# A four-layer scan network on one core: products of the preparation copied out one unit later, layer 1's steps at other units, and the product with C written over h in a ring of seven

## The chip, the cores and the metric

The kernel runs on one core of a Trainium2 chip. The time is that of the device, in microseconds (us), from the first to the last instruction of the core. A shorter time is better. The numbers before the change are the median of three runs; durations of single instructions come from one further execution taken by the hardware profiler.

Five engines work side by side, each through its own queue of instructions: TensorE (PE in the profile; PEld is its weight load), VectorE (DVE), ScalarE (ACT), GpSimd (POOL) and SyncE (SP), which here only issues transfers. An engine that must wait for another waits on a semaphore.

## What is computed

The input is x of shape (4, 64, 64, 192) in float32. Four layers are applied, each as x = x + layer(group norm of x). Layers 0 and 3 are two-dimensional state-space scans in four directions over 4096 positions of an image, layer 2 is a pair of Toeplitz products, and layer 1 holds four independent one-dimensional scans over lines of 64 positions: along rows and along columns, each forwards and backwards. The scan of layer 1, which is the part that the change touches most:

```python
def mamba_block(xs, in_w, cw, cb, xw, dtw, dtb, Alog, Dv, ow):
    N, L, _ = xs.shape
    xz = jnp.einsum('nlc,dc->nld', xs, in_w)
    u, z = jnp.split(xz, 2, axis=-1)
    ...
    uc = jax.lax.conv_general_dilated(u_pad, cw[:, None, :], (1,), 'VALID', feature_group_count=DI)
    uc = silu(uc + cb[None, :, None])
    ...
    x_dbl = jnp.einsum('nld,ed->nle', uc, xw)
    dt, Bp, Cp = jnp.split(x_dbl, [DT_RANK, DT_RANK + DS], axis=-1)
    delta = jax.nn.softplus(jnp.einsum('nlr,dr->nld', dt, dtw) + dtb)
    A = -jnp.exp(Alog)

    def step(h, inp):
        d_t, b_t, c_t, u_t = inp
        dA = jnp.exp(d_t[:, :, None] * A)
        h = dA * h + (d_t * u_t)[:, :, None] * b_t[:, None, :]
        y = jnp.einsum('nds,ns->nd', h, c_t)
        return (h, y)
    ...
    y = jnp.moveaxis(ys, 0, 1) + uc * Dv
    y = y * silu(z)
    return jnp.einsum('nld,cd->nlc', y, ow)
```

There are 384 inner channels (192 in layer 3) and 16 states for each. Layers 0 and 3 run the same recurrence over a whole image, after a two-dimensional convolution.

## The kernel before

**Jobs and units.** A job is one chunk of 512 positions of one image in one direction. Layers 0 and 1 have 128 jobs each, layer 3 has 128 of half the channels. A job is cut into units: 64 channels times 4 states fill 128 partitions with 2 x 512 values each. That gives 24 units a job in layers 0 and 1 and 12 in layer 3, 7680 in all. `TWO` and `ONE` give the order of the units (channel tile t, group of states p, half c).

**What a unit costs.** TensorE spreads (delta times u) times B into PSUM (tile `b`, line 351), from a transposed copy `dtuT` and diagonal matrices `diag` that ScalarE makes (line 305). ScalarE makes `dA` by two exponentials (line 374). VectorE runs the recurrence (line 384 in layer 1, two scans at line 391 in layers 0 and 3) into `h`. GpSimd multiplies `h` by C into `hc` (line 396). TensorE adds the states of `hc` into `y` in PSUM (line 414, four matmuls a unit, in two halves for each pair of units). For a few units, called direct (p = 3), GpSimd makes b itself (`bs`, line 324) in place of TensorE, and `dA` is written to PSUM.

**The order.** `run_jobs` writes out a program in steps i, one for each unit. In step i it feeds unit i + 2 (`feed`: b and dA), scans unit i (`scan`: recurrence, product with C, and in layers 0 and 3 a copy of the last column to `carry`), spreads B for direct unit i + 3, folds an earlier pair (`collect`), and then calls whatever `steps` holds for i. A scheduler turns the program into a fixed order for each engine, and an engine takes its instructions in that order. So an instruction that waits holds up all behind it on its engine.

**The steps** prepare the next jobs. Their places are counted from the job's first unit, so in layer 1 the step -24 falls on the first unit of the job before. In layer 1 a job has these: `load` (the chunk xn by SP, and a buffer for u), three `input_of` (product for u, first tap on ScalarE at line 778, three taps on VectorE at line 783, Silu on ScalarE at line 786), `project` (B, C and the rank of dt into `xd`, then to memory), `turn_b`, three `step_size` (delta before Softplus, line 249), `finish` (Softplus, line 253, and delta times u, line 254), `store`, three `turn` (transposes into dtuT, line 268), three `gate` (z with Silu, line 791), and two `out`. Each makes a product on TensorE in one of two PSUM buffers (`mm`) and has ScalarE or VectorE copy it out at once, in the same step. `gated` (lines 800 and 801) follows the last fold of a channel tile. ScalarE holds one table of functions; Exp, Silu and Softplus are here in three, so each Silu or Softplus between two exponentials costs two table loads.

**Buffers that matter.** `h` has 3 buffers and `hc` 5; `dA` has 3; `b` has 2 in PSUM; `mm` has 2; xn has 2 and u has 3. `plan` places the loads of C, B, delta and delta times u, up to 12 units ahead of their first reader, not before a unit at which their source is ready.

Of the kernel before, what the change touches and what calls it, by code (L numbers as in the profile page):

```python
# [19 lines left out]
T = 512  # L20
# [16 lines left out]
class Kernel:  # L37
# [66 lines left out]
    def run_jobs(self, jobs, pools):  # L104
# [15 lines left out]
        waiting = []  # L120
        for i in range(min(start, -EARLY), end):
# [4 lines left out]
            if 0 <= i < len(units):  # L126
                k, t, p, c = units[i]
                self.scan(jobs[k], t, p, c, pools)
# [9 lines left out]
            if todo:  # L138
                k, two, n = waiting.pop(0)
                self.collect(jobs[k], two, n, pools)  # L140
                if n and two[1][1] == LAST:
                    jobs[k]["add"](two[0][0])
            for step in steps.get(i, []):
                step()

    def plan(self, jobs, order, pools):
# [3 lines left out]
        for k, job in enumerate(jobs):  # L150
# [6 lines left out]
            for j, (t, p, c) in enumerate(order):  # L157
                i, g = k * len(order) + j, 2 * t + c
                direct = c in job["direct"].get(p, ())
                reads = [("c", p, i, when["project"] + 5), ("both", g, i - AHEAD, when["finish"] + near)]  # L160
                if direct:
                    reads += [("bc", p, i - EARLY, when["project"] + 5), ("dtu2", g, i - EARLY, dtu)]
                else:
                    reads.append(("diag", p, i - AHEAD, when["turn_b"] + 5))
# [26 lines left out]
    def prepare(self, job, pools):  # L191
# [4 lines left out]
        def project():  # L196
# [3 lines left out]
            for t in range(NT):  # L200
                for h in range(2):
# [3 lines left out]
                    )  # L205
            xd = job["xd"] = prep.tile([128, 256], F32, name="xd", bufs=1)
# [23 lines left out]

        def turn_b():
# [5 lines left out]
            nc.scalar.copy(bt.rearrange("p (h k) n -> p k h n", h=2), of)  # L237

        def step_size(t):
# [9 lines left out]
            nc.scalar.activation(job["delta"][:, t, :], dp[:P], AF.Identity, bias=w["dtb"][:, t : t + 1])  # L249

        def finish():
            delta = job["delta"]
            nc.scalar.activation(delta, delta, AF.Softplus)  # L253
            (nc.gpsimd if job["carry"] is None else nc.vector).tensor_mul(job["dtu"], delta, job["u"])  # L254
            if job["carry"] is not None:
                return
            job["deltas"] = self.bcd.tile([DI, T], F32, name="delta_dram")
            nc.scalar.dma_start(job["deltas"].rearrange("(t p) l -> p t l", p=P), delta)

        def turn(t):  # L260
# [3 lines left out]
            if P == 128:  # L264
                to = job["dtuT"][t] = prep.tile([128, NB, P], F32, name="dtuT", bufs=NT + 1)
            else:
                to = job["dtuT"][:, :, t * P : (t + 1) * P]
            nc.scalar.copy(to, ps)
# [108 lines left out]
    def scan(self, job, t, p, c, pools):  # L377
# [4 lines left out]
        h = pools["work"].tile([128, 2 * T], F32, name="h", bufs=3)  # L382
        if carry is None:
            nc.vector.tensor_tensor_scan(h[:, way], dA[:, way], b[:, way], 0.0, ALU.mult, ALU.add)  # L384
        else:
# [8 lines left out]
            nc.scalar.copy(carry[g, p], hn[:, :, 0 if rev else T - 1])  # L394
        hc = pools["work"].tile([128, 2 * T], F32, name="hc", bufs=5)
        nc.gpsimd.tensor_mul(hc, h, job["cbc"][p])  # L396
        job["done"][t, p, c] = hc

# [124 lines left out]
    def ss2d_scan(self, pre, u_d, y_d, P, NT, ways, A, dtb):  # L523
# [3 lines left out]
        with (  # L527
# [27 lines left out]
            for k, (col, rev) in sorted(enumerate(ways), key=lambda one: one[1]):  # L555
# [7 lines left out]
                for c in range(NCH - 1, -1, -1) if rev else range(NCH):  # L563
# [11 lines left out]
                    def add(t, job=job, col=col, rev=rev, s=s):  # L575
                        y, rows = job["y"][t], min(128, DI - t * 128)
                        if rows == 64:

                            both = work.tile([128, T], F32, name="out", bufs=3)
                            nc.scalar.copy(both, y)  # L580
                            y = mm.tile([64, T], F32, name="fold_ps", tag="mm")
                            nc.tensor.matmul(y, self.fold, both, start=True, stop=True)
                        out = work.tile([rows, T], F32, name="out", bufs=3)
                        if rev:
                            nc.vector.tensor_add(out, y, job["before"].pop(t))
                        else:
                            nc.scalar.copy(out, y)
                        nc.scalar.dma_start(y_d[col][t * 128 : t * 128 + rows, s], out)
# [151 lines left out]
    def mamba_job(self, pw, pin, mm, i, begin, rev, w, x, done, both_w, c, fixed, zero):  # L740
# [33 lines left out]
        def input_of(t):  # L774
# [3 lines left out]
            nc.scalar.activation(u, ps, AF.Identity, scale=tap(3))  # L778
            for j in range(1, 4):
                to, of = slice(j, HW), slice(0, HW - j)  # L780
                if rev:
                    to, of = of, to
                nc.vector.scalar_tensor_tensor(  # L783
                    u[:, :, to], ps[:, :, of], tap(3 - j), u[:, :, to], ALU.mult, ALU.add
                )
            nc.scalar.activation(u, u, AF.Silu, bias=w["conv_b"][:, t : t + 1])

        def gate(t):
            if t == 0:
                job["z"] = pin.tile([P, NT, T], F32, name="z")  # L790
            nc.scalar.activation(job["z"][:, t, :], project(t, DI, "z"), AF.Silu)
# [6 lines left out]
        def gated(t):  # L798
            u, z = job["u"][:, t, :], job["z"][:, t, :]
            nc.vector.scalar_tensor_tensor(u, u, w["D"][:, t : t + 1], job["y"][t], ALU.mult, ALU.add)  # L800
            nc.gpsimd.tensor_mul(z, z, u)
# [15 lines left out]
        def out(m):  # L817
# [9 lines left out]
            if rev:  # L827
                nc.vector.tensor_add(o, ps, o)
            else:
                nc.scalar.copy(o, ps)  # L830
            for rows, ch, at in parts(m):
                nc.sync.dma_start(done[ch, at], o[rows, :])

        when = dict(project=-24, turn_b=-22, step_size=(-20, -18, -17), finish=-15, turn=(-10, -7, -3), store=-11)
        each = lambda f, ats: [(at, lambda t=t: f(t)) for t, at in enumerate(ats)]
        steps = [(-50, weights)] if begin else []
        steps += [(-48, load)] + each(input_of, (-45, -32, -29)) + each(gate, (-6, -4, -2)) + each(out, (32, 35))
        if rev:
            steps += each(earlier, (26, 29))
# [328 lines left out]
```

## Time and profile before

| | us |
|---|---|
| median of three runs | 31623.03 |
| lowest and highest | 31622.8 and 31625.03 |
| the profiled execution | 31644.44 |
| its span, from first to last instruction | 31641.4 |
| layer 0: scans of one image (four of them) | 2270 |
| layer 1: all jobs | 11520 |
| layer 3: scans of one image (four of them) | 1285 |

The last three rows are stretches of the profiled execution. The rest of the span belongs to the inputs and outputs of layers 0 and 3 and to layer 2 (about 22290 to 25290), which the change leaves alone. A line of groups in the profile gives line, engine, operation, tiles and shapes, then the number of instructions; after the bar come the time in which the group was busy, the mean duration of one in ns, and the idle time of the engine just before them with what ended it. A line of waits gives who waited for whom: us in total, times, and the longest.

### The profile page before, as it was taken

To read this page: it belongs to the slowest core of one execution; us is meant where nothing else is said; L and a number is where in the kernel's file an instruction comes from. 1 tells how busy PE (TensorE), PEld (TensorE's weight loads), DVE (VectorE), ACT (ScalarE), POOL (GpSimd) and SP (SyncE) were. 2 spreads that over 40 slices of the span, in tenths; PEclk is the share of its full clock that TensorE was granted. 3 is DMA by queue.
4 is the path that set the end of the run, shared out by engine and by line. 5 is a ranking of instruction groups with operands and counts; after the bars stand their busy time and mean duration, and the time that the engine had idled before them with its cause. 6 is when DMAs were issued, how large, how long until landed. Compare 5 with 4: busy or idle time off the path is not lost.

```text
span 31641.4 us, 503746 instructions
## 1 busy us (share of the span) xinstructions
PE 27491.3 (87%) x189464; PEld 16459.4 (52%) x189464; DVE 22376.5 (71%) x16587; ACT 23377.2 (74%) x50388; POOL 22882.0 (72%) x9831
## 2 busy tenths in 40 slices
PE   8998998998899689888888998888588988888888
PEld 5654654665565355555555555555355344444444
DVE  7887887888888677776667777666423267777767
ACT  7885885886788488888878888878232187878777
POOL 7885885886788388888888888888100077777777
PEclk9999999999999899999999999999788999999999
DMA  3333334334333433333333333323533444444444
GB/s 107 103 98 115 103 99 119 99 97 112 106 101 99 135 95 95 95 96 93 95 95 95 94 94 96 94 93 94 129 78 77 104 128 126 128 126 129 126 129 125
DMA packets 1606619, 3342.23 MB, mean 106 GB/s; under 512 B 350645, under 2 KB 407414, under 8 KB 1588566
## 3 DMA queue, kind: packets, MB, share of 16 engines
q1 hardware_dynamic: 1432150, 3033.08, 35.4%
q10 hardware_dynamic: 172032, 276.92, 2.6%
q8 instruction: 1497, 24.53, 0.3%
q14 instruction: 940, 7.70, 0.1%
HBM read 2149.81 MB, written 656.08 MB: 89 GB/s over the span
## 4 chain that ended last, share of the span: by engine, by line
PE 32%; ACT 20%; DVE 15%; POOL 15%; DMA 9%; issue 8%; SPq 1%; ACTq 1%; DVEq 0%; POOLq 0%
PE b L351 12%; POOL hc L396 11%; ACT diag L305 7%; DVE h L391 7%; PE y L414 6%; ACT dA L374 5%; DVE h L384 3%; DMA xn<-m_col 2%; DMA xn<-m_row 2%; POOL bs L324 2%; PE yt_ps L1018 2%; ACT b L374 2%; DMA xn<-t_xn 2%; PE conv_ps L500 2%; POOL dtu L254 1%
## 5 line engine op out<-in xcount | busy, mean ns | idle before, releaser
L396 POOL TENSOR_TENSOR hc<-h,c 128x1024 f32<-128x1024 f32 x7680 | 18152.7, 2385 | 3279.0 <-DVE h L384 1520.9
L351 PE MATMUL b<-diag,dtuT 128*64 128x256 f32 x98304 | 13293.5, 389 | 1212.0 <-DVE h L391 720.5
L351 PEld LDWEIGHTS b<-diag,dtuT 128*64 128x64 f32 x98304 | 8701.4, 139 | 5531.3 <-issue 1840.9
L414 PE MATMUL y<-hc,fold 128*64 128x512 f32 x30720 | 10297.8, 604 | 918.1 <-POOL hc L396 896.8
L391 DVE TENSOR_TENSOR_SCAN h<-dA,carry,b 128x512 f32<-128x512 f32 x6720 | 8183.8, 1264 | 1482.5 <-PE b L351 779.6
L374 ACT ACTIVATE dA<-both,A 128x512 f32<-128x512 f32 (+1 forms) x12288 | 8333.1, 712 | 567.7 <-DVE h L384 551.8
L384 DVE TENSOR_TENSOR_SCAN h<-dA,b 128x1024 f32<-128x1024 f32 x2304 | 5244.7, 2282 | 2214.7 <-PE b L351 1011.0
L305 ACT ACTIVATE diag<-ident,bt 128x128 f32<-128x128 f32 x20480 | 6503.3, 390 | 138.6 <-issue 104.0
L414 PEld LDWEIGHTS y<-hc,fold 128*64 128x64 f32 x30720 | 3121.3, 138 | 3147.3 <-POOL hc L396 1904.1
L324 POOL TENSOR_TENSOR bs<-dtu,bc 128x1024 f32<-128x1024 f32 x1536 | 3640.1, 2370 | 169.7 <-DMA dtu<-dtu 73.0
L468 POOL MEMSET pad<- 128x13068 f32 (+1 forms) x8 | 73.4, 9172 | 3972.6 <-DMA cw<-in_L_conv_w 3003.3
L374 ACT ACTIVATE b<-both,A 128x504 f32<-128x504 f32 (+1 forms) x3072 | 2079.1, 677 | 368.8 <-DVE h L391 324.4
L384 DVE TENSOR_TENSOR_SCAN h<-b,bs 128x1024 f32<-128x1024 f32 x768 | 1752.9, 2282 | 287.9 <-ACT b L374 177.7
L394 ACT COPY carry<-h 128x2 f32<-128x2 f32 x4608 | 846.3, 184 | 1292.8 <-DVE h L391 1092.3
L391 DVE TENSOR_TENSOR_SCAN h<-b,carry,bs 128x512 f32<-128x512 f32 x1344 | 1640.8, 1262 | 210.7 <-ACT b L374 108.1
L783 DVE SCALAR_TENSOR_TENSOR u<-in_ps,conv_w,u 128x504 f32<-128x504 f32 (+2 forms) x1152 | 829.5, 720 | 946.4 <-ACT u L778 929.8
L226 PEld LDWEIGHTS dtu_ps<-ident,dtu 128*64 128x64 f32 (+1 forms) x16384 | 1185.7, 140 | 559.9 <-issue 283.7
L374 ACT ACT_TABLE_LOAD x1125 | 1443.4, 1283 | 18.2 <-DMA both<-delta_dram 4.0
L226 PE MATMUL dtu_ps<-ident,dtu 128*64 128x128 f32 (+1 forms) x16384 | 1374.4, 274 | 64.1 <-DVE dtu L254 41.6
L766 PE MATMUL in_ps<-xn,in_w 96*64 96x512 f32 x3072 | 1052.8, 626 | 390.5 <-DMA xn<-m_row 199.1
L391 DVE TENSOR_TENSOR_SCAN h<-dA,b 128x512 f32<-128x512 f32 x960 | 1113.7, 1205 | 363.3 <-ACT dA L374 134.5
L254 DVE TENSOR_TENSOR dtu<-delta,u 128x1536 f32<-128x1536 f32 (+1 forms) x256 | 571.3, 2232 | 572.4 <-ACT delta L253 572.2
(154 smaller groups left out, 23411.3 us busy)
## 6 DMA issues: line engine op xcount, KB each, us to landing
c<-bc_dram SPq DMA_DIRECT2D x3072, 256.0 KB
both<-delta SPq DMA_DIRECT2D x2048, 128.0 KB
bc<-bc_dram SPq DMA_DIRECT2D x768, 256.0 KB
both<-delta_dram SPq DMA_DIRECT2D x768, 256.0 KB
dtu<-dtu_dram SPq DMA_DIRECT2D x768, 256.0 KB
dtu<-dtu SPq DMA_DIRECT2D x1280, 128.0 KB
L_y<-out ACTq DMA_DIRECT2D x512, 256.0 KB
u<-L_u SPq DMA_DIRECT2D x160, 768.0 KB
```

The source lines that it names most:

```text
L226: nc.tensor.matmul(to[half * 64 : (half + 1) * 64], of[:, half * 64 : (half + 1) * 64], self.ident[:p, :p], start=True, stop=True,)
L254: (nc.gpsimd if job["carry"] is None else nc.vector).tensor_mul(job["dtu"], delta, job["u"])
L305: nc.scalar.activation(to, self.ident, AF.Copy, scale=of)
L324: self.nc.gpsimd.tensor_mul(by(b), dtu, by(job["bbc"][p]))
L351: nc.tensor.matmul(to, dtu, job["diag"][p][:, k, 2 * q : 2 * q + 2, :], start=True, stop=True,)
L374: nc.scalar.activation(to[n], of, AF.Exp, scale=w["A"][:, g, 2 * p + n : 2 * p + n + 1])
L384: nc.vector.tensor_tensor_scan(h[:, way], dA[:, way], b[:, way], 0.0, ALU.mult, ALU.add)
L391: nc.vector.tensor_tensor_scan(hn[:, n, way], dA[:, n, way], by_n[:, n, way], start, ALU.mult, ALU.add)
L394: nc.scalar.copy(carry[g, p], hn[:, :, 0 if rev else T - 1])
L396: nc.gpsimd.tensor_mul(hc, h, job["cbc"][p])
L414: nc.tensor.matmul(y[c * 64 : (c + 1) * 64, :], self.fold, of, start=first == 0 and n == 0, stop=last == LAST and n == 1)
L766: nc.tensor.matmul(ps[half * 64 : (half + 1) * 64, :], w["in_w"][:, k, first : first + 64], job["xn"][:, k, :], start=k == 0, stop=k == KC ...
```

## The change

1. A step may return a function, and `run_jobs` calls that one unit later. The steps of the preparation make their product in one unit and return the copy that takes it out of PSUM (in `input_of` the taps come one unit later, and the Silu one more). The carry copy of layers 0 and 3, the add of a finished y, and delta times u also move by one unit. `plan` counts C and B as ready one unit later.
2. In layer 1 the places change: `load` from -48 to -46, `input_of` from (-45, -32, -29) to (-37, -34, -31), `step_size` from (-20, -18, -17) to (-20, -19, -17), `turn` from (-10, -7, -3) to (-9, -2, 3), `gate` from (-6, -4, -2) to (-4, -1, 1), `out` from (32, 35) to (30, 33), `earlier` from (26, 29) to (25, 28).
3. In layer 1 the product with C is written over `h`, which has a ring of seven; `hc` with its five buffers is gone there. In layers 0 and 3 `h` and `hc` stay.

```diff
-        waiting = []
-        for i in range(min(start, -EARLY), end):
+        waiting, rest = [], []
+        for i in range(min(start, -EARLY), end + 4):
...
-                self.scan(jobs[k], t, p, c, pools)
+                after = self.scan(jobs[k], t, p, c, pools)
+                if after is not None:
+                    steps.setdefault(i + 1, []).insert(0, after)
...
-                    jobs[k]["add"](two[0][0])
-            for step in steps.get(i, []):
-                step()
+                    steps.setdefault(i, []).append(lambda job=jobs[k], t=two[0][0]: job["add"](t))
+            now, rest = rest + steps.pop(i, []), []
+            for step in now:
+                after = step()
+                if after is not None:
+                    rest.append(after)
...
             nc.scalar.activation(delta, delta, AF.Softplus)
-            (nc.gpsimd if job["carry"] is None else nc.vector).tensor_mul(job["dtu"], delta, job["u"])
...
+            def after():
+                (nc.gpsimd if job["carry"] is None else nc.vector).tensor_mul(job["dtu"], delta, job["u"])
+
+            return after
...
-        h = pools["work"].tile([128, 2 * T], F32, name="h", bufs=3)
+        h = pools["work"].tile([128, 2 * T], F32, name="h", bufs=7 if carry is None else 3)
...
-            nc.scalar.copy(carry[g, p], hn[:, :, 0 if rev else T - 1])
-        hc = pools["work"].tile([128, 2 * T], F32, name="hc", bufs=5)
+        hc = h if carry is None else pools["work"].tile([128, 2 * T], F32, name="hc", bufs=5)
         nc.gpsimd.tensor_mul(hc, h, job["cbc"][p])
         job["done"][t, p, c] = hc
+        if carry is None:
+            return None
+
+        def after():
+            nc.scalar.copy(carry[g, p], hn[:, :, 0 if rev else T - 1])
+
+        return after
...
+                        def halves():
                             both = work.tile([128, T], F32, name="out", bufs=3)
                             nc.scalar.copy(both, y)
...
+                            def sum_them():
+                                one = mm.tile([64, T], F32, name="fold_ps", tag="mm")
+                                nc.tensor.matmul(one, self.fold, both, start=True, stop=True)
+                                return lambda: last(one)
+
+                            return sum_them
+
+                        return halves if rows == 64 else last
...
-            nc.scalar.activation(u, ps, AF.Identity, scale=tap(3))
...
+            def taps():
+                nc.scalar.activation(u, ps, AF.Identity, scale=tap(3))
...
+                return last
+
+            def last():
+                nc.scalar.activation(u, u, AF.Silu, bias=w["conv_b"][:, t : t + 1])
+
+            return taps
...
-            nc.scalar.activation(job["z"][:, t, :], project(t, DI, "z"), AF.Silu)
+            ps = project(t, DI, "z")
+
+            def after():
+                if t == 0:
+                    job["z"] = pin.tile([P, NT, T], F32, name="z")
+                nc.scalar.activation(job["z"][:, t, :], ps, AF.Silu)
+
+            return after
...
-        when = dict(project=-24, turn_b=-22, step_size=(-20, -18, -17), finish=-15, turn=(-10, -7, -3), store=-11)
+        when = dict(project=-24, turn_b=-22, step_size=(-20, -19, -17), finish=-15, turn=(-9, -2, 3), store=-11)
...
-        steps += [(-48, load)] + each(input_of, (-45, -32, -29)) + each(gate, (-6, -4, -2)) + each(out, (32, 35))
+        steps += [(-46, load)] + each(input_of, (-37, -34, -31)) + each(gate, (-4, -1, 1)) + each(out, (30, 33))
         if rev:
-            steps += each(earlier, (26, 29))
+            steps += each(earlier, (25, 28))
```

## The prediction, made before the changed kernel had run

> **What bounds the kernel now.** I read the page first, then busy time in windows (one per layer), then the groups and the waits inside layer 1, then one job of layer 1 in order of time.
>
> ```profile
> span 31641.4 us, 503746 instructions
> PE 27491.3 (87%) x189464; PEld 16459.4 (52%) x189464; DVE 22376.5 (71%) x16587; ACT 23377.2 (74%) x50388; POOL 22882.0 (72%) x9831
> ```
>
> No engine fills the span, so the answer lies in the stages. The next lines are three windows: one of the four images of layer 0's scans, all of layer 1's, one image of layer 3's. Columns: window, length, busy time of PE, PEld, DVE, ACT, POOL, then granted clock, DMA share, GB/s.
>
> ```profile
> 189.00:2459.00 2270.00, 2121.34 (x16633) 1364.42 (x16629) 1957.55 (x1614) 1906.68 (x4711) 2017.30 (x863) 0.97 0.38 98
> 10770.00:22290.00 11520.00, 10195.31 (x69976) 6136.16 (x69974) 7978.45 (x4719) 9458.56 (x17176) 9860.38 (x4360) 0.97 0.30 94
> 25448.00:26733.00 1285.00, 1130.64 (x8130) 665.49 (x8126) 996.68 (x829) 1173.16 (x3002) 1146.79 (x479) 1.00 0.50 129
> ```
>
> Layer 1 is the largest single stage: 11520 us, 128 jobs, 90.0 us a job of 24 units. Its POOL is busy 9860 us, 77.0 a job, and idles 1660 us, 13.0 a job. Where that idle time comes from, by groups (first line) and by waits (the rest):
>
> ```profile
> L396 POOL TENSOR_TENSOR hc<-h,c 128x1024 f32<-128x1024 f32 x3072 | 7214.8, 2371 | 1598.2 <-DVE h L384 1520.9 <-DMA c<-bc_dram 64.4 <-PE b L351 7.2
> ...
> DVE h L384 <- PE b L351: 1011.0, 389, 11.7
> ACT u L778 <- PE in_ps L766: 923.6, 241, 14.2
> DVE u L783 <- ACT u L778: 898.5, 268, 14.6
> ...
> DVE h L384 <- POOL hc L396: 609.6, 417, 5.4
> ...
> DVE h L384 <- ACT dA L374: 538.8, 191, 8.7
> ```
>
> POOL waits for nothing but late scans. The scans are late because DVE stands behind a convolution tap (L783) that waits for ACT (L778), which waits for TensorE's product, or because dA is late on ACT. Yet DVE also waits 609.6 us for POOL: at other places it could run further ahead and the ring of three h forbids it. One job of POOL in order of time (start, length, what, in brackets the idle time before it) shows that the idle time is not spread:
>
> ```profile
> 16175.02 2.37 POOL L396 TENSOR_TENSOR hc<-h,c 128x1024 f32<-128x1024 f32 x1 [5.14 <-DVE h L384]
> ...
> 16190.50 2.36 POOL L396 TENSOR_TENSOR hc<-h,c 128x1024 f32<-128x1024 f32 x1 [3.81 <-DVE h L384]
> ...
> 16207.06 2.38 POOL L396 TENSOR_TENSOR hc<-h,c 128x1024 f32<-128x1024 f32 x1 [6.04 <-DVE h L384]
> ...
> 16214.62 11.69 POOL L396 TENSOR_TENSOR hc<-h,c 128x1024 f32<-128x1024 f32 x5
> ```
>
> These are units 21, 1 and 4; from unit 5 to unit 20 POOL never stops (five multiplies in 11.69 us, 2.34 each). Averaged over 124 jobs the idle time before POOL's work is 4.35 us at unit 21, 0.58 + 2.73 + 0.68 at units 0, 1 and 2 (and 0.41 before the gated multiply there), 3.29 + 0.45 at units 4 and 5, 0.20 at 9 and 10: 12.7 a job. So layer 1 is POOL-bound for two thirds of a job and has three holes in the rest.
>
> **What the skill says.** The Trainium skill, "ScalarE: Activation LUTs", section "What ACT_TABLE_LOAD costs", gives about 1283 ns for a table load and 1380 ns of drain. The trace agrees on the first (1283 in every load group) and shows no drain behind it: a load at 16257.88 of 1.28 us is followed by dA at 16259.17. "Perfetto Trace Analysis", section "Tensor Engine Instruction (MATMUL, LD_WEIGHTS)", says ACT, DVE and GpSimd take their instructions strictly in order; the 898.5 us of scans held behind L783 agree. "TensorE: Matmul & The Clock Gate", section "What's actually happening", says an array idle for some 3.4 us falls to half clock. At 16199.38 the first matmul after 4.10 us of waiting for xn takes 1.09 us where 0.59 is usual, so a DMA wait costs more than itself.
>
> **The change part by part.** The built order of both programs (it holds no times) tells what moves.
>
> 1. Chunk loaded 9 units ahead. Before, xn was loaded 3 units before its first product, about 11 us, and took 13.2 to 16.7 us in the chains. PE waited 376 us for it directly (190.5 + 185.3), and unit 4's hole is its shadow. After, load at unit 2 and product at unit 11: nine units at 3.3 us, 30 us. No byte is added; SP issues the same load one unit after the last product that reads the old chunk, so it blocks nothing new. 3.74 us a job fall to about 0.1: -3.6.
>
> 2. Steps spread. An excursion of ACT to another table costs two loads and the work: 2 x 1.28 + 0.60 to 0.72 = 3.2 us, six a job and one for Softplus (4.0). Before, in a job of the second direction, five stood between dA of unit 22.5 and 1.5 of the next job. In those three units ACT owed 16 us for them, 4.2 for dA (3 x 1.4), some 3.5 for diag and 1.2 for copies, 25 us, while POOL needed about 9. The 15 us of shortage less the lead (three dA buffers, 7 to 9 us) leave 6 to 8 us; the measured holes at 21 and 0 to 2 are 8.75. After, the excursions stand at 19, 21, 23 or 0, 2 or 3, and 5. Over those 10.5 units ACT owes 16 + 14.7 + 2.8 (copies) + 7.5 (diag), 41 us; POOL owes 10.5 x 2.34 + three bs at 2.33 + two z at 1.24, 34 us. Shortage 7, about the lead. Silus share a load somewhat more often: 2334 loads in all for 2395, 61 x 1.28 = 78 us of ACT, inside the lead. The first tap used to be ordered such that DVE waited for an ACT 1.5 to 2.5 units ahead; now 2.5, 1.5 and 0.5. I leave 1.0 of 4.35 at unit 21 and 2.0 of 4.40 at units 0 to 2: -5.7. Bounds: nothing regained, and all 8.75.
>
> 3. Evacuation in the next unit. 923.6 us of ACT and 898.5 of DVE idle in layer 1 are the same holes as in 1 and 2, so they are not counted again. Each product holds its PSUM buffer (two of them) a unit longer; products are at least a unit apart, so the third finds the first one free. Bounds: -0.5 to +1 us a job, taken at 0. The gated step and POOL's dtu (3.41 us) also move by one unit.
>
> 4. Ring of seven. The five hc buffers go and the scan of unit u+7 waits for TensorE's fold of unit u instead of the scan of u+3 for POOL's multiply of u. In the built order that fold comes after b of u+6 at the latest, which needs the scan of u+4, so it stands two scans clear. It lets DVE lead POOL by about four units instead of three, 2.3 us more cover at each hole; that is what makes the 1.0 and 2.0 above plausible. No work is added. Cost taken at 0.
>
> Second floor. TensorE's matmuls, counts by mean spacing in layer 1, owe 79.5 us a job (b 34.2, y 21.2, products for u and z 11.1, the rest 13.0). Part of that is the cold clock: granted 0.97, so 3% or 2.5 us, most of it behind the xn waits that go. That leaves some 77, as much as POOL's. Two engines in strict order that meet at every fold will not both be full: 0.7 us a job is given back.
>
> Layer 1: 3.6 + 5.7 - 0.7 = 8.6 us a job x 128 = -1100 us, 81.4 us a job against 77.0 of POOL.
>
> 5. Layers 0 and 3. In layer 0 the built order hardly changes: the scheduler already put the copies behind later dA, the DVE order is the same to the instruction, and its one hole (DVE's dtu behind Softplus at unit 11) stays. The carry copy moves behind dA of u+3, but that dA waits for the same scan (three dA buffers), so 256.9 us an image of ACT waiting for it mostly change their name: -20 in all. In layer 3 the halves' fold and last add move by one to three units; DVE waited 43.4 us an image for y and ACT 38.8 behind that. Half of the first: -20 x 4 = -80. Bounds for both layers: +150 to -350.
>
> Sum: -1100 - 20 - 80 = -1200. The profiled execution took 31644 us (span 31641.4 and 3 around it), so 30444; it lay 21 above the median of 31623, so **30420 us**.
>
> **Rivals.** (A) Only the DMA hole closes, because ACT's shortage of 7 us in a row uses up the lead and shows later: 3.6 x 128 = -460, and nothing elsewhere: 31160. For it: ACT's total work is not less. Against: POOL pauses for no ACT over units 5 to 20, where Softplus stands. (B) POOL never starves: 12.5 x 128 = -1600 and -200 in layers 0 and 3: 29820. Against: the second floor. (C) The ring makes it slower: the fold is the second half of a pair and queues behind b (1.73 us) and the first half (0.86), so DVE waits up to 2.6 us at each of 12 pairs. Above 0.7 us a pair this eats the whole gain; at 1.0, 12.0 - 8.6 = +3.4 x 128 less 100 elsewhere: 31960. For it: PEld already waits 893.3 us for hc at the fold. Against: the built order's clearance. (D) The scheduler undoes the spreading: no change. Against: the order shows it moved.
>
> **How the numbers follow.** Forecast 0.58 (30050 to 30800 for itself), A 0.20, B 0.12, C 0.07, D 0.03. The range leaves out C, D and the far edges of A and B: 29900 to 31080. Faster 0.90; within 0.2% (63 us, about what a measurement of this kernel can tell from none) 0.03; slower 0.07.
>
> **What would show it.** Right: in layer 1 POOL's idle time before its multiply falls from 1598 to about 550 us, PE waits for xn no more, the table-load groups of L374, L786 and L791 lie apart, a window of 1000 us there has POOL over 930, and layers 0 and 3 keep their lengths within 1%. Step 1 is wrong if a hole stays at unit 4; step 2 if holes move to units 14 to 16 behind Softplus; step 4 if scans wait for y. The prediction is wrong as a whole if layer 0 changes by more than 2%, since I give its order no effect.

## The result and the profile after

The kernel after takes 31289.92 us (median of 4; before 31624.03), a ratio of 0.9894 with a 95% interval of 0.9877 to 0.9911. The direction was forecast; the size was not: 334 us in place of 1200. The profiled execution has a span of 31282.5 us.

The windows of the kernel after, in the same three stages as before (columns: window, length, busy time of PE, PEld, DVE, ACT, POOL, granted clock, DMA share, GB/s):

```profile
189.00:2459.00 2270.00, 2110.20 (x16571) 1366.54 (x16567) 1948.03 (x1607) 1898.23 (x4702) 2009.32 (x859) 0.97 0.37 98
10794.00:21995.00 11201.00, 10189.22 (x69942) 5865.06 (x69942) 7953.58 (x4717) 9352.71 (x17118) 9860.85 (x4359) 0.97 0.31 97
25156.00:26427.00 1271.00, 1106.57 (x8137) 663.17 (x8134) 994.66 (x830) 1174.92 (x3002) 1149.32 (x480) 0.99 0.49 131
```

GpSimd (POOL) and TensorE are as busy in layer 1 as before; only idle time went. Measured from the first to the last multiply by C, the four images of layer 0 take 9115.0 us in sum (before 9080.3), layer 1 11188.6 (11507.3), layer 3 5072.6 (5142.4): +35, -319 and -70. All layer times below are read in this way. A job of layer 1 is timed from its first multiply to that of the next job, as the mean of 30 inner jobs of each way: the forward ways take 85.2 us a job (87.5 before), the backward ways 89.5 (92.1).

GpSimd's groups in layer 1, after; the idle time before each and its end stand behind the bar:

```profile
L418 POOL TENSOR_TENSOR h<-h,c 128x1024 f32<-128x1024 f32 x3072 | 7209.3, 2376 | 918.1 <-DVE h L407 570.0 <-DMA c<-bc_dram 284.0 <-PE b L374 26.9
L347 POOL TENSOR_TENSOR bs<-dtu,bc 128x1024 f32<-128x1024 f32 x768 | 1821.2, 2371 | 307.9 <-issue 224.8 <-DMA dtu<-dtu_dram 80.2 <-DMA c<-bc_dram 1.4
```

The multiply's idle time fell from 1598 to 918, where about 550 was forecast. The share that ends with a scan fell from 1521 to 570. But C's transfers now end 284 us of it (64 before), and the product bs, which hardly waited before (24 us), waits 308. The waits of layer 1 (us in total, times, longest) name the rest:

```profile
PEld y L443 <- POOL h L418: 1208.6, 704, 19.9
DVE h L407 <- PE b L374: 829.2, 688, 9.1
DVE h L407 <- ACT b L397: 790.9, 418, 3.1
...
DVE u L852 <- PE y L443: 659.2, 127, 10.8
...
ACT dA L397 <- DMA bc_dram<-xd: 337.4, 54, 8.4
ACT dtuT L289 <- PE dtu_ps L235: 286.4, 77, 5.3
```

No wait of TensorE for the chunk is left. In its place VectorE waits for dA of the direct units (b L397, 179 before), for the fold in the gate's sum (95 before), and ScalarE for transfers and for TensorE. One backward job of GpSimd in order of time shows where (start, length, idle time in brackets):

```profile
14510.68 4.72 POOL L418 TENSOR_TENSOR h<-h,c 128x1024 f32<-128x1024 f32 x2
14521.19 2.37 POOL L347 TENSOR_TENSOR bs<-dtu,bc 128x1024 f32<-128x1024 f32 x1 [5.80 <-issue]
14523.52 9.27 POOL L418 TENSOR_TENSOR h<-h,c 128x1024 f32<-128x1024 f32 x4
14536.60 1.27 POOL L853 TENSOR_TENSOR z<-z,u 128x512 f32<-128x512 f32 x1 [3.81 <-DVE u L852]
14540.01 2.36 POOL L418 TENSOR_TENSOR h<-h,c 128x1024 f32<-128x1024 f32 x1 [2.14 <-DMA c<-bc_dram]
```

The old holes at units 21, 1 and 4 closed, and others opened at 21 (before bs), 1 (before z) and 2. Over 30 jobs of a way: backward 4.4 us at unit 21 and 5.4 at unit 2; forward 1.4 at z of unit 1, 1.5 at unit 2, 4.6 at units 6, 7 and 9.

### The profile page after: what moved, and what is told of

Read it like the earlier page. It is cut to its first block, busy times and chain, and to the rows that moved or that the text cites. A ratio compares the mean times of both kernels' runs of the same rounds, so it can differ in the third digit from the quotient of the medians.

```text
span 31282.5 us, 503240 instructions
## 1 busy us (share of the span) xinstructions
PE 27353.4 (87%) x189464; PEld 16218.5 (52%) x189464; DVE 22344.0 (71%) x16587; ACT 23257.2 (74%) x50327; POOL 22884.2 (73%) x9831
## 5 line engine op out<-in xcount | busy, mean ns | idle before, releaser
L418 POOL TENSOR_TENSOR hc<-h,c 128x1024 f32<-128x1024 f32 x4608 | 10938.8, 2394 | 1641.9 <-DVE h L414 1336.6
L374 PEld LDWEIGHTS b<-diag,dtuT 128*64 128x64 f32 x98304 | 8544.2, 139 | 5362.7 <-issue 1770.1
L397 ACT ACTIVATE dA<-both,A 128x512 f32<-128x512 f32 (+1 forms) x12288 | 8308.5, 711 | 2062.3 <-DVE h L414 981.2
L418 POOL TENSOR_TENSOR h<-h,c 128x1024 f32<-128x1024 f32 x3072 | 7209.3, 2376 | 918.1 <-DVE h L407 570.0
L443 PE MATMUL y<-hc,fold 128*64 128x512 f32 x18432 | 5587.0, 605 | 534.0 <-POOL hc L418 533.3
L443 PE MATMUL y<-h,fold 128*64 128x512 f32 x12288 | 4736.9, 614 | 716.2 <-POOL h L418 713.0
L443 PEld LDWEIGHTS y<-hc,fold 128*64 128x64 f32 x18432 | 1709.8, 139 | 1684.1 <-POOL hc L418 978.7
L397 ACT ACTIVATE b<-both,A 128x504 f32<-128x504 f32 (+1 forms) x3072 | 2074.0, 675 | 527.9 <-DVE h L414 438.3
L443 PEld LDWEIGHTS y<-h,fold 128*64 128x64 f32 x12288 | 1321.9, 139 | 1804.2 <-POOL h L418 1210.7
L235 PE MATMUL dtu_ps<-ident,dtu 128*64 128x128 f32 (+1 forms) x16384 | 1309.6, 278 | 171.2 <-ACT z L839 125.3
```

Of the source, the lines that this page charges most:

```text
L235: nc.tensor.matmul(to[half * 64 : (half + 1) * 64], of[:, half * 64 : (half + 1) * 64], self.ident[:p, :p], start=True, stop=True,)
L374: nc.tensor.matmul(to, dtu, job["diag"][p][:, k, 2 * q : 2 * q + 2, :], start=True, stop=True,)
L397: nc.scalar.activation(to[n], of, AF.Exp, scale=w["A"][:, g, 2 * p + n : 2 * p + n + 1])
L443: nc.tensor.matmul(y[c * 64 : (c + 1) * 64, :], self.fold, of, start=first == 0 and n == 0, stop=last == LAST and n == 1)
```

## Experiments: the parts alone

Each run below is one part of the change alone, or the change without one part. Late evacuation means that a product is copied out of PSUM one unit later. Theory A: the change does what the forecast's steps say, and new waits at the new places take the gain. B: the ring couples VectorE to the fold. C: another part carries the gain (three h were short, or late evacuation).

e1_ring, the kernel before with

```
-        h = ... name="h", bufs=3)
+        h = ... name="h", bufs=7 if carry is None else 3)
-        hc = ... name="hc", bufs=5)
+        hc = h if carry is None else ... name="hc", bufs=5)
```

> The kernel before, with one part of the change alone: in layer 1 the product with C is written over h, in one ring of seven; places and evacuations stay old. Theory A (the change's gain was lost to new waits at the new places; the ring is neutral): all layers within 0.2%, layer 1 11507 +- 25 us, total 31560 to 31690. Theory B (the ring of seven couples VectorE to TensorE's fold, so scans wait for the fold): layer 1 longer by 100 us or more, total above 31720, and VectorE waits for y in layer 1. Theory C (h was short at three, the wait of VectorE for GpSimd, 610 us in the profile before, was real): layer 1 shorter by 150 us or more.

e2_places, the kernel before with the new `when`, `steps` and `earlier` numbers of layer 1 and nothing else:

> The kernel before, with layer 1's new places alone (chunk loaded 46 units ahead of its first scan and its first projection at 37, steps spread, out and earlier two or one units sooner); each product is still evacuated in its own unit, h and hc stay apart. Theory A (places take the old holes away and open new ones): layers 0 and 3 unchanged within 3 us an image; layer 1 shorter by 150 to 300 us; TensorE no longer waits for the chunk (376 us before), holes at units 2 and 21 of the backward ways appear. Theory B (ring at fault): layer 1 shorter by 450 us or more here, since the ring is absent. Theory C (late evacuation carries the gain): layer 1 changes by less than 100 us.

e3_late, the kernel after with those numbers and h, hc put back:

> The kernel after, with layer 1's old places and h (three) and hc (five) apart: of the change only the evacuation in the next unit is left, in all layers. Theory A: layer 0 longer by 35 us in sum and layer 3 shorter by 70 us in sum, as in the kernel after, since only this part touches them; layer 1 shorter by 0 to 150 us; total 31450 to 31600. Theory C (late evacuation carries layer 1's gain): layer 1 shorter by 250 us or more, total below 31360. Against both: layer 1 longer than before.

e4_noring, the kernel after with h (3) and hc (5) put back:

> The kernel after, with h (three) and hc (five) apart in layer 1: places and late evacuation stay, the ring is undone. Theory A (ring neutral): total 31260 to 31340, layer 1 within 40 us of 11189. Theory B (the ring holds the scans back): layer 1 shorter by 150 us or more, total below 31140. Theory C (three h were short): layer 1 longer by 150 us or more.

Measured (us; total is the median):

| kernel | total | layer 0 | layer 1 | layer 3 | forward / backward us a job |
|---|---|---|---|---|---|
| before | 31624 | 9080 | 11507 | 5142 | 87.5 / 92.1 |
| e1_ring | 31610 | 9075 | 11477 | 5146 | 87.2 / 91.9 |
| e2_places | 31240 | 9078 | 11106 | 5143 | 84.0 / 89.7 |
| e3_late | 31445 | 9112 | 11348 | 5068 | 88.3 / 88.8 |
| e4_noring | 31329 | 9109 | 11243 | 5067 | 86.2 / 89.4 |
| after | 31290 | 9115 | 11189 | 5073 | 85.2 / 89.5 |

Layer times come from one profiled execution each, and that of the kernel before lay 21 us above its median; beside the four runs the kernel before took 31613. The ring alone is therefore not told from none: -31 us in layer 1 of the profile, but 31610 against 31613 in the medians. Beside the rest it brings -54. B and the ring's half of C fall. The places are worth -401. Late evacuation is worth -159 alone and **+137** on top of the places (e4 less e2). So the places alone beat the whole change, by 50 us in total and 83 in layer 1. e3's waits in layer 1 say why the two don't add:

```profile
ACT u L818 <- PE in_ps L804: 604.5, 229, 10.2
...
PE in_ps L804 <- DMA xn<-m_col: 211.5, 59, 9.1
PE in_ps L804 <- DMA xn<-m_row: 207.1, 55, 12.0
```

TensorE still waits 419 us for the chunk there, but ScalarE's wait for the product fell from 924 to 605 and VectorE's behind it from 899 to 507; the backward ways lose 3.3 us a job. Both parts take the hole at unit 4 (it is closed in e2 and in e3); together they take it once, and late evacuation's own price (+0.8 us a job in e3's forward ways, +2.2 in e4's against e2's) stays.

## Experiments: the queue of the backward ways, and the gate

f1_split, the kernel after with

```
-            o = job["o"][m] if rev else pin.tile(..., name="o")[:, : T >> m]
+            res = pin.tile([128, T], F32, name="res")[:, : T >> m]
...
-                    nc.vector.tensor_add(o, ps, o)
+                    nc.vector.tensor_add(res, ps, job["o"][m])
...
-                    nc.sync.dma_start(done[ch, at], o[rows, :])
+                    nc.sync.dma_start(done[ch, at], res[rows, :])
```

> The kernel after, with the sum of the two halves of the output in a tile of its own (res), so that the next job's load of the earlier half waits for VectorE's read of o and not for the landing of the store just ahead of it in the same queue. Theory S (the holes of the backward ways, POOL idle 4.4 us at unit 21 and 5.4 at unit 2 of a job, are that queue standing still behind one store): SyncE's wait of the load for the store (389 us in 14000:16000) goes, the backward ways fall by 3 to 5 us a job, from 2866 and 2848 us by 100 to 160 each, the forward ways (2742, 2733) stay within 15; total 30970 to 31090. Rival (the queue is late for other reasons, C's or dtu's buffers come free late): the wait goes and the holes stay; total within 60 of 31290.

SyncE's waits in layer 1, first the kernel after, then f1_split:

```profile
SPq L869 <- DMA m_out<-o: 1068.1, 126, 14.0
```

```profile
SPq L869 <- DMA m_out<-res: 36.3, 30, 13.1
```

The total is 31010, layer 1 10915, backward ways 84.9 us a job, forward 85.3. Theory S is shown: with res, a tile of its own for the sum, the wait is gone and the backward ways are shorter. The scheduler puts the next job's load of the earlier half directly behind the store that frees its buffer, so SyncE stood 8.5 us (1068 by 126) until that store had landed, with the loads of C, dtu and both behind it. The wait is older than the change; in the kernel before it was

```profile
SPq L815 <- DMA m_out<-o: 807.7, 133, 8.8
```

g1_gated (the gate's two products at once again, in `gated`) and g2_nosilu (`AF.Silu` to `AF.Identity` in `gate`; the gate's function is left out):

> The kernel after, with the gate's two products of layer 1 (VectorE u, GpSimd z) recorded in the unit in which y is complete, as before; all else late. Theory G (GpSimd and VectorE wait at unit 1 for TensorE's fold because this product is recorded a unit later, right between the scans): the hole at z, unit 1, 1.4 us in the forward ways, and part of the 1.55 at unit 2 go, the forward ways fall by 1 to 2 us a job (2742, 2733 by 30 to 65 each); total 31170 to 31250. Rival (the products wait for the fold wherever they stand): within 40 of 31290.

> The kernel after, with the gate's Silu left out in layer 1 (Identity in its place), so that ScalarE loads no function table for it; everything else as after. It measures what the gate's excursions, now at units -3, 0 and 2 of a job, cost. Theory X (ScalarE's excursions now stand ahead of dA for units 2 and 5, whose scans wait 3 us each for them, and TensorE's cold restart follows): about 6 loads a job fewer (7.7 us of ScalarE), the holes at units 1 to 9 of the forward ways fall from 8 to below 4 us a job, layer 1 falls by 400 to 600 us. Theory F (TensorE's own work, 79.6 us busy a job of 87.4, is the floor): layer 1 falls by less than 150 us.

g1 gave 31285, and VectorE's wait for the fold stayed at 654 us: the scheduler put the product in nearly the same place. So it tests little. g2 gave 31259: layer 1 26 us less for some 900 us less of busy ScalarE. Its groups of GpSimd:

```profile
L418 POOL TENSOR_TENSOR h<-h,c 128x1024 f32<-128x1024 f32 x3072 | 7207.3, 2370 | 1016.0 <-DMA c<-bc_dram 657.3 <-DVE h L407 255.0 <-PE b_ps L235 69.6
L347 POOL TENSOR_TENSOR bs<-dtu,bc 128x1024 f32<-128x1024 f32 x768 | 1821.1, 2371 | 311.6 <-DMA dtu<-dtu_dram 201.7 <-issue 103.9 <-POOL h L418 5.0
```

The scans' share fell from 570 to 255, as theory X says, and C's transfers took it over (284 to 657). In the forward ways a job falls from 85.2 to 84.2 us, in the backward ways it grows from 89.5 to 90.5. X's amount is refuted, and F's reason is not borne out: the wait that took over is a transfer, not TensorE.

## Experiments: a better version, and where the floor is

h1_combo: new places, ring and res; evacuation at once in layers 0 and 1 (where C and B then count as ready one unit sooner again), late in layer 3:

```
             for step in now:
                 after = step()
+                while after is not None and not pools["late"]:
+                    after = after()
...
```

> New places, ring of seven and res apart in layer 1; evacuation in its own unit in layers 0 and 1, in the next unit in layer 3 alone. If the parts add (places -401 and ring -31 to -54 in layer 1, late evacuation -73 in layer 3 and +35 avoided in layer 0, the split store another -200 to -320): layer 1 10720 to 10900, layer 0 as before (9080), layer 3 5070; total 30830 to 31010. If the split does nothing: about 31110. If late evacuation is needed beside the split (it shortened the backward ways at the old places): 31010 to 31100.

30850.77 us, ratio 0.9758 (0.9742 to 0.9774). Layer 1 is 10793, 122 less than f1_split. The parts add.

Three edits on top of it in layer 1, with other parts of late evacuation in layers 0 and 3. i1_half: `for k in range(KC)[:1]` in `project`, which leaves out half of the products for u and z. i2_dve: `nc.vector.tensor_mul(job["dtu"], ...)`. i3_bcsp: `nc.sync.dma_start(by_half[h], ...)`.

> Three stages, three questions, all on top of h1_combo. Layer 1: the second half of the contraction over the chunk's channels is left out in the products in_ps and z_ps (half of 48 multiplies a job, 1831 us of TensorE in the layer, so about 915 us less). If TensorE's own work is the floor that stopped the gain: layer 1 shorter by 500 us or more than h1_combo's 10793. If the floor is elsewhere (GpSimd, 77.1 us a job, and its hand-over with VectorE): shorter by less than 200. Layer 0 and 3: everything late but the copy of the carry. If that copy made layer 0 slower (9115 after, 9081 before): layer 0 is 9075 to 9090; if another evacuation did: 9105 to 9120. If that copy made layer 3 faster: 5130 or more; if the others did: 5060 to 5085.

> On top of h1_combo. Layer 1: dtu = delta times u by VectorE in place of GpSimd (3.46 us x 128 = 443 us less on GpSimd, which is then 73.7 us a job; VectorE takes it up, 1.6 to 2.4 us a job, with 27 per cent of its time free). If GpSimd is the bound where it does not idle: layer 1 shorter by 200 to 440 us. If the hand-over of scans decides (VectorE waits for TensorE and ScalarE at units 2 and 9): within 100 of 10793. Layers 0 and 3: the copy of the carry late, all else in its own unit: layer 0 9105 to 9120 and layer 3 5130 or more if that copy costs in layer 0 and brings nothing in layer 3; layer 0 9075 to 9090 if it is not the cause.

> On top of h1_combo. Layer 1: the two stores of bc issued on SyncE's queue in place of ScalarE's, so that ScalarE does not stand before dA and diag while an issue waits for an older transfer (169 + 24 us of its waits end with a load of C or both). If these waits make the direct units' dA late: layer 1 shorter by 100 to 250 us, the hole at unit 2 (3.0 to 3.9 us a job) falls by a third or more. If SyncE's queue, which must now wait for xd, makes C late instead: layer 1 longer, GpSimd waits more for C than 216 us.

i1: TensorE's work falls and layer 1 becomes 102 us longer (10896). i2: 10923, also longer. i3: 10840; ScalarE's waits for transfers go (one of 10 us is left) and GpSimd's wait for C rises from 216 to 466, the miss that the expectation named. Less work of TensorE (busy 9600 us for 10023) does not shorten layer 1. i1 is not a clean test, since the order of ScalarE's instructions changed with the products and brought 162 more table loads, some 207 us. In i2 GpSimd has less to do and idles more, 10.0 us a job against 7.3, in a job that is no shorter; but i2 carries a second effect (last section). Neither engine's work is seen to be the floor.

Which part of late evacuation costs? On h1_combo, in layer 1: i4_prep has only `prepare`'s steps late, j2_taps only `input_of`, j3_gate only `gate`.

> On top of h1_combo. Layer 1: of the late evacuations only those of the preparation's products (xd, bt, delta, dtu, dtuT) are put back; the input's taps, the gate, the sum and the output stay in their own unit. If these are what costs beside the new places (ScalarE waits for dtu's products 286 us in the kernel after, for nothing in h1_combo): layer 1 longer by 60 to 140 us than 10793. If the gate, the taps or the sum are: within 30 us of it.

> On h1_combo. Layer 1: only the input's taps and Silu late (the gate, the sum, the output and the preparation at once). If the taps give back the 122 us (10915 in f1_split, 10793 in h1_combo): 10860 or more; if not: 10760 to 10820. Layers 0 and 3: only the preparation's evacuations late: if they bring the gain, layer 3 4920 to 4945 and layer 0 9070 to 9080; if the sum does, 5140 and 9082.

> On h1_combo. Layer 1: only the gate's Silu late. If the gate gives back the 122 us (its Silu then stands ahead of dA for the direct units 2 and 5): 10860 or more; if neither this nor j2's taps do, the sum or the output does. Layers 0 and 3: only the sum's step (the two halves' fold and out) late: layer 3 5140 if the preparation brings the gain, 4931 if the sum does.

Layer 1: 10789, 10790 and 10834. The preparation and the taps cost nothing, the gate 40; the other 82 lie in the sum, the output or the parts together, which was not tried. Layers 0 and 3, from the same runs:

| late there | layer 0 | layer 3 |
|---|---|---|
| nothing (before) | 9080 | 5142 |
| all (after) | 9115 | 5073 |
| carry alone (i2) | 9109 | 5158 |
| all but the carry (i1) | 9074 | 4931 |
| preparation alone (j2) | 9074 | 5125 |
| sum alone (j3) | 9062 | 5002 |

The carry's copy is the whole loss of layer 0. In layer 3 it costs 141 us beside the other late parts (all less all but the carry) but 16 alone (i2 less before); the sum's step (the fold of the halves) alone brings 140. The waits show the copy: one image of layer 3, first the kernel after, then i1_half.

```profile
DVE h L414 <- ACT carry L424: 138.8, 133, 3.6
```

```profile
DVE h L430 <- ACT carry L440: 1.6, 1, 1.6
```

Three h turn in these layers; a copy that reads h a unit later holds the buffer that a scan needs. In layer 0 this wait is 43.0 us an image after and 7.4 before.

## Experiments: what stays open

j1_best: h1_combo with five tiles of C in layer 1 (`dict(c=5, ...)`; o and res cut to size, one buffer for each half) and all but the carry late in layers 0 and 3. j4_c5nosilu: the same without the gate's Silu. k2_bufs: j1_best with `dtu2=4`, a ring of six (to make room), and in layer 0 only the sum's step late. k1_all: k2_bufs with g2's and i1's omissions.

> h1_combo with two edits. Layer 1: five tiles of C in place of four (o and res cut to the size each half needs, to make room). A job uses four tiles of C, so with four the next job's second tile can be loaded only between its last use at unit 21 and its first at unit 26; with five it has seven units more. If that window makes the hole at unit 2 (3.0 to 3.9 us a job): GpSimd's wait for C (216 us) goes, layer 1 falls by 150 to 400 us below 10793. If the scans behind ScalarE make it: layer 1 within 80 of 10793, the hole stays with VectorE as its end. Layers 0 and 3: all evacuations late but the carry's copy, as in i1_half: 9074 and 4931. Total in the first case 30300 to 30560, in the second 30630 to 30790.

> j1_best with the gate's Silu left out in layer 1 (Identity in its place), as in g2_nosilu beside the kernel after. There the loads' loss brought 26 us, since C came late at unit 2 in their place. If the two hide each other, both gone: layer 1 shorter than j1_best's by 300 us or more (below 10400), the holes of units 1 to 9 below 3 us a job. If a third thing holds them (the two tiles of PSUM through which TensorE, ScalarE and VectorE hand on): within 150 of j1_best.

> Layer 1: five tiles of C, four of dtu2, a ring of six (to make room), res apart, everything evacuated in its own unit; and left out: the gate's Silu (Identity instead) and the second half of the contraction in in_ps and z_ps. If several limits lie close together and each hid the others: layer 1 falls to 10500 or less (82 us a job or less, GpSimd idle below 5). If the hand-over TensorE to VectorE to GpSimd through two tiles of PSUM sets the pace whatever the rest: 10700 to 10900. Layer 0: only the sum's step late, 9062; layer 3: all late but the carry's copy, 4931.

> k1_all without what it leaves out: five tiles of C, four of dtu2, a ring of six, res apart; layers 0 and 3 as there. If transfers that come late for want of buffers set the pace: layer 1 10400 to 10650, total 30280 to 30550. If not: layer 1 10760 to 10860, total 30640 to 30760. Against both: the ring of six holds the scans back, layer 1 above 10900.

j1_best is the best: 30730.37 us, 0.9721 (0.9705 to 0.9737). But its gain on h1_combo is layer 3's (4935); layer 1 is 10812. GpSimd's groups in layer 1 of h1_combo, then j1_best, then j4_c5nosilu (layer 1: 10823):

```profile
L428 POOL TENSOR_TENSOR h<-h,c 128x1024 f32<-128x1024 f32 x3072 | 7215.9, 2372 | 919.0 <-DVE h L417 644.9 <-DMA c<-bc_dram 216.2 <-DVE u L862 15.0
L357 POOL TENSOR_TENSOR bs<-dtu,bc 128x1024 f32<-128x1024 f32 x768 | 1819.3, 2369 | 34.1 <-DMA dtu<-dtu_dram 30.7 <-issue 2.6
```

```profile
L434 POOL TENSOR_TENSOR h<-h,c 128x1024 f32<-128x1024 f32 x3070 | 7205.9, 2371 | 684.8 <-DVE h L423 475.8 <-PE z_ps L820 59.6 <-PE b_ps L251 51.6
L363 POOL TENSOR_TENSOR bs<-dtu,bc 128x1024 f32<-128x1024 f32 x768 | 1819.1, 2369 | 283.4 <-DMA dtu<-dtu_dram 223.5 <-issue 47.9 <-POOL h L434 11.1
```

```profile
L434 POOL TENSOR_TENSOR h<-h,c 128x1024 f32<-128x1024 f32 x3071 | 7200.0, 2370 | 410.4 <-DVE h L423 319.0 <-DMA c<-bc_dram 57.2 <-PE y L459 28.9
L363 POOL TENSOR_TENSOR bs<-dtu,bc 128x1024 f32<-128x1024 f32 x768 | 1820.1, 2370 | 585.1 <-DMA dtu<-dtu_dram 503.4 <-issue 45.8 <-DMA bc<-bc_dram 33.6
```

C's wait goes with the fifth buffer, as expected, yet the sum of the two idle times is 953, 968 and 996: it moves from the scans to C, from C to dtu, and stays. k2_bufs is worse (31208, layer 1 11291), k1_all too (31139, 11223). Their edits are mixed; in k2_bufs VectorE waits 396 us for the multiply (95 in h1_combo) and ScalarE 595 for a load of both before diag (20). They show that more buffers of dtu with a smaller ring don't help; they don't name the floor. What holds layer 1 at 83.7 to 85.4 us a job in h1_combo, j1_best and j4_c5nosilu is **not settled** by a run.

The traces hold a strong candidate, which none of these runs changes: two of the 16 DMA engines. A trace records each update of a transfer's landing counter. A load of C (256 KB) in layer 1 of the kernel after has 16 updates: the 14th comes 3.6 us after the issue and the last 11.6 (medians). For the chunk xn these are 3.8 and 12.1. The loads of both and dtu, also 256 KB each and twelve a job, have three: one 0.4 us after the issue and two at the end, 14 to 15 us after it. While no other transfer of layer 1 is under way, 2.1 packets are in flight on average. So I read it that two engines carry these loads whole, and that their share of every other transfer queues behind. In layers 0 and 3, where both and dtu are loaded by rows of 64, the same loads have 16 updates; in layer 1 their source has two copies as its outermost dimension (`broadcast_to([2, 64, T])`), C's has 64.

| layer 1 of | part of the time with a load of both or dtu under way | that time, us a job |
|---|---|---|
| before | 92.4% | 83.1 |
| after | 97.0% | 84.9 |
| f1_split | 99.1% | 84.5 |
| h1_combo | 99.6% | 84.0 |
| j1_best | 99.7% | 84.1 |

In h1_combo these loads end 7.0 us apart on average where the next is already issued, and 12 x 7.0 = 84 us is the length of its job (10793 by 128 = 84.3). That fits a sum of idle times that only changes its name. The DMA share of h1_combo, the second column from the right, hides it, since it is a mean over 16 engines:

```profile
10770.00:21600.00 10830.00, 10033.82 (x69978) 5707.13 (x69978) 7968.23 (x4723) 9261.67 (x17059) 9870.09 (x4360) 0.98 0.33 100
```

No run spreads these loads over more engines, so this is an inference from the traces and not a shown cause.

## Why the prediction was wrong

Layer 1 was to lose 1100 us and lost 319. Of the 781 that are missing, f1_split brings 273 and evacuation at once (h1_combo) another 122; 386 stay, and for these there is only the candidate above.

- **Step 1, the chunk (-3.6 us a job): right in its mechanism.** TensorE's 376 us of waiting are gone, and the hole at unit 4 with them. What this brings in time is not separated from step 2 by a run of its own. The hole was 5.5 us a job in the backward ways and 1.0 in the forward ways, which the average over all jobs hid.
- **Step 2, steps spread (-5.7): the term that failed.** Steps 1 and 2 together were to bring 9.3 us a job; e2_places, which is these two with the small moves of `out` and `earlier`, brought 401 by 128 = 3.1. The forecast priced a hole by ScalarE's shortage of work and let the rest of it vanish. The runs gave new ends to the idle time: the direct units' dA, C's transfer, dtu's. Taking ScalarE's gate loads away altogether (g2) brought 0.2 us a job. The named sign of failure, holes at units 14 to 16, did not come; they came at 1, 2, 6 to 9 and 21.
- **What no step had:** the transfers. Behind one store SyncE's queue holds the loads of a backward job up, for 4.6 us a job (f1_split against after), and step 1, which said that the chunk's load "blocks nothing new", treated xn as the only transfer at stake. The wait stands in the kernel before too (808 us); what it cost there was not run. And the forecast's 81.4 us a job lies below the 83 to 85 us for which loads of both and dtu are under way in every kernel of the table above; the sum named 77.0 of GpSimd and some 77 of TensorE as its floors.
- **Step 3, late evacuation (0, bounds -0.5 to +1): the value was wrong, the bound nearly held.** On top of the places it costs 137 by 128 = 1.1 us a job.
- **Step 4, the ring (0): right.** It brings nothing clear alone and 0.4 us a job beside the rest; scans wait 4 us for the fold in the whole layer. Rival C falls.
- **Second floor (0.7 given back): its reason is not borne out.** With half of two products left out the layer got no shorter.
- **Step 5:** layer 3 -70 for -80, right in sum by luck, since it is made of a gain of 211 and a loss of 141 that the step did not see. Layer 0 +35 for -20: it said the copy's later place would only rename a wait; the copy holds one of three h. Layer 0 stayed inside the 1% that was named (+0.4%), layer 3 did not (-1.4%).
- Rival A (31160, only the transfer's hole closes) came nearest in its number, 130 us below the result. Its reason, ScalarE's shortage showing later, holds at most in part: g2 takes the gate's table loads away and brings 26 us.

## What to carry to other kernels

When a stage idles for several reasons, the hole that a releaser ends is at best an upper bound of what removing it brings (scans ended 570 us here, and g2, which takes away what made many of them late, brought 26): look for what is next late there (the loads, their queue, the buffers) and price the hole at the difference. Look also at how the parts of a transfer land, since a small mean share of 16 DMA engines does not say that none of them is full. Before a load that waits for a buffer is queued behind a store that frees it, give the two different tiles; one such wait delays every load behind it. And when a step is put off, list the buffers that it reads: a late reader costs where the ring is short, here three deep.

## What was not expected of the hardware

An issue of a transfer can stop the engine that issues it. ScalarE's waits that end with a transfer grew from 12 us in layer 1 before to 399 after and some 930 in k2_bufs, and nearly all stand just behind its two issues of the store of bc. For 337 us of the kernel after the profile names that store itself. The counters of the trace say otherwise. Eight landing counters serve the transfers of both issuing engines, and ScalarE's issue leaves when the transfer before it on its counter has fully landed: all 117 delayed issues in layer 1 left within 0.1 us of that counter's last update. Of the 328 us that ScalarE stood before them, 289 belong to loads of C that SyncE had issued (10 us in all in the kernel before). So ScalarE waits for the last parts of SyncE's loads. i3_bcsp, which takes these issues from ScalarE, leaves 10 us of such waits; counters for ScalarE alone were not run.

The product dtu took 3646 ns on VectorE (i2_dve), not less than GpSimd's 3469, and GpSimd's multiply rose from 2372 to 2433 on average. That is the 127 multiplies that overlap such a product, 3855 ns each; the others stay at 2372. The Trainium skill, "GPSIMD Engine Reference", section "1. Specifications", says that GpSimd shares its SBUF interfaces with VectorE's instructions that have two SBUF inputs, which this product is. The run agrees: moving it gave VectorE a slow instruction that also delays GpSimd, and my 1.6 to 2.4 us for it was wrong.
